# Channel sums of a two-layer banded kernel: four classes of 32 channels on the array's column quarters instead of two halves of 64

## Chip, cores and metric

The kernel runs on one core of a Trainium2 chip. The metric is device time in microseconds (us) of one execution; lower is better. "Before" is the median of three runs.

## What is computed

Input x has 512 x 512 positions with 64 channels, fp32. Two layers of the same kind follow each other, each adding its result to its input. Cut to what matters:

```python
def _gn(v, G=32, eps=1e-5):            # groups of two channels
    g = v.reshape(B_, H_, W_, G, C_ // G)
    m = jnp.mean(g, axis=(1, 2, 4), keepdims=True)
    s = jnp.var(g, axis=(1, 2, 4), keepdims=True)
    return ((g - m) / jnp.sqrt(s + eps)).reshape(v.shape)

# one layer, on xn = _ln(_gn(x)) with 64 channels, HID = 128
left  = (xn @ Wl + bl) * mask * sigmoid(xn @ Wlg + blg)
right = (xn @ Wr + br) * mask * sigmoid(xn @ Wrg + brg)
out_gate = sigmoid(xn @ Wog + bog)
out = _banded_ingoing(left, right, 4)  # 9 products per output, along one axis
out = _ln(out) * out_gate
x = x + (out @ Wo + bo)
```

`_gn` needs, for each of 32 groups of two channels, the mean and the variance over all 512 x 512 positions. For the second layer these are statistics of the first layer's output, and the second layer can't begin before they are complete.

## The kernel before, in words

The 512 rows are cut into nine overlapping blocks of 64 (`row_blocks`), the other axis into chunks; a **unit** (`Unit`, `Out`) is 64 rows by 8 positions of either half of the axis, so that 128 partitions hold two halves. There are 288 units a layer, 8 to a **period**, 36 periods. Before the first layer `input_stats` reads the whole input once on VectorE for the first `_gn`, while the weights are prepared (`solve_layer`, `save`).

A unit goes through some thirty **steps**: `load`, `scale`, `move` (the affine map of `_gn`), `inner` and the steps to `resc` (the layer norm), `ztr`, `keep` (transposes on TensorE, copies on ScalarE), `proj`, `sig`, `right` (projections and their gate), `band` (the banded products, `mix`), `copy`, `ost`, `norm`, `turn`, `gate`, `gated`, `tg` and `last` (`end`, the product with Wo), then `end` (the addition to x in tile XR), `stp` (store) and, in the first layer alone, `sums`. The order in which the engines get the steps of a period is written out by hand in the tables `FIRST` (line 39, first layer) and `SECOND` (line 69); every engine works in the order of its program. In `FIRST` stand eight `sums` steps, one per unit of the period.

`sums` (line 902) adds each finished unit to the statistics of the first layer's output, without leaving TensorE: the tile XR (line 1231) holds, for each of up to 128 partitions (one row of one half), four pairs of neighbouring positions, 2 x 64 channels each, with a column of ones on either side (`clear_xr`, line 1234; `fetch`, line 865, places the data between them). The matrix product of the 64 channels of one position with themselves and the ones has the sums of squares on its diagonal and the channel sums in the column of ones. It accumulates over all units in one PSUM tile, `acc` (line 1242): positions of even place in its lower 64 partitions, of odd place in the upper 64. A unit is 4 x 2 fp32 matmuls with contraction over the rows, 64 stationary columns and 65 moving columns:

```python
acc[t * D : (t + 1) * D], lhsT=o.xr[:n, k, 1 + t * D : 1 + (t + 1) * D],
rhs=o.xr[:n, k, t * (D + 1) : (t + 1) * (D + 1)],
```

The profile's rows count each fp32 matmul as two records of a matmul, with a weight load (LDWEIGHTS) to each; a transpose is one record.

After the first layer `mid_stats` (line 1134) takes the diagonal and the sums out of `acc`, adds the part of the bias bo (`bo_col`, loaded in `save`, line 1182), sums the partitions of one group by a matmul with the tile `same` (line 202), and makes the affine map of the second layer's `_gn`.

Of the kernel before, what the change touches and what calls it, by code (L numbers as in the profile page):

```python
# [10 lines left out]
F32 = mybir.dt.float32  # L11
# [3 lines left out]
ALU = mybir.AluOpType  # L15
# [4 lines left out]
P = 128  # L20
# [4 lines left out]
JU = 8  # L25
# [5 lines left out]
NX = 6  # L31
# [2 lines left out]
NB = 32  # L34
GN_EPS = 1e-5
LN_EPS = 1e-6
UP = (1024.0 / 27.0) ** 2

FIRST = """
# [77 lines left out]
def col(v: bass.AP) -> bass.AP:  # L117

    return v.rearrange("(p o) -> p o", o=1)
# [38 lines left out]
def tile_two_banded_layers(  # L158
# [6 lines left out]
    nc = tc.nc  # L165
    _, L, _, D = x.shape
# [7 lines left out]
    sm = ctx.enter_context(tc.tile_pool(name="sm", bufs=2))  # L174
# [19 lines left out]
    ident = const.tile([P, P], F32, name="ident")  # L194
# [3 lines left out]
    ln_eps = const.tile([P, 1], F32, name="ln_eps")  # L198
    nc.vector.memset(ln_eps, LN_EPS * UP)
    ones_row = all_ones[:1]  # L200

    same = const.tile([P, D], F32, name="same")
    nc.vector.tensor_tensor(same, ident[:, :D], ident[:, D:], ALU.add)
    pair = const.tile([P, G], F32, name="pair")
    nc.vector.tensor_reduce(pair, same.rearrange("p (g t) -> p g t", t=2), AX.X, ALU.add)
    nc.vector.tensor_scalar(
# [8 lines left out]
    def any_bank():  # L215
        return two_banks(next(turns))[:, :512]
# [59 lines left out]
    def strided(v: bass.AP, at: int, *dims) -> bass.AP:  # L276

        return bass.AP(tensor=v.tensor, offset=v.offset + at, ap=[list(d) for d in dims])
# [35 lines left out]
    def solve_layer(i: int, f: dict, r: dict, tmp, half: bass.AP):  # L314
# [67 lines left out]
        en.vector.tensor_tensor(r["m2"], r["m"], r["m"], ALU.mult)  # L382
        en.vector.tensor_scalar(r["m2"], r["m2"], UP / H, None, ALU.mult)

# [13 lines left out]
    bo = [const.tile([P, D], F32, name="bo0"), None]  # L398
    bo_col = const.tile([P, 1], F32, name="bo_col")
# [7 lines left out]
    def group_affine(mean: bass.AP, var: bass.AP, pool):  # L407

        ve = pool.tile([P, D], F32, name="g_ve")
        nc.vector.tensor_scalar(ve, var, GN_EPS, None, ALU.add)  # L410
        rsqrt(ga, ve, pool)
        nc.vector.scalar_tensor_tensor(gb, mean, -1.0, ga, ALU.mult, ALU.mult)
# [328 lines left out]
    def solve(w: dict, ins: list, outs: list, sti, sto) -> tuple:  # L741
# [19 lines left out]
        def prepare():  # L761
            held.extend((work[0], temporary("var")))
            bank, v = held
            if ni:
                en.scalar.activation(
                    pairs(v[:, :ni]), sti[:, : ni // 2, 2::3], AF.Identity, bias=ln_eps,
                    scale=UP / D,
                )
# [7 lines left out]
        def seed():  # L776
            bank, v = held
            y = bank[:, :n]
            if no:
                vo = bank[:, 6 * NB : 6 * NB + no]  # L780
                vec.tensor_tensor(vo, vo, w["m2"][:, js], mult)
                vec.tensor_scalar(v[:, ni:], vo, LN_EPS * UP, None, add)

# [77 lines left out]
    def rows_of(v: bass.AP, o: Out, e: int):  # L861
        b, j = o.blk, e * LH + o.j
        return v[b.s + b.lo : b.s + b.hi, j : j + JU, :].rearrange("p (k t) c -> p k (t c)", t=2)

    def fetch(src: bass.AP, o: Out, n: int, stats: bool):
        o.xr = XR[n % NX]
        if stats:
            o.f = o.xr[:, :, 1 : 1 + 2 * D]
        else:
            o.f = o.xr.rearrange("p k c -> p (k c)")[:, : JU * D].rearrange("p (k c) -> p k c", c=2 * D)  # L870
        for e in range(2):
            en.sync.dma_start(o.f[e * S : e * S + o.blk.m], rows_of(src, o, e))
# [29 lines left out]
    def sums(o: Out, first: bool, final: bool):  # L902


        n = S + o.blk.m
        for k in range(JU // 2):
            for t in range(2):
                en.tensor.matmul(
                    acc[t * D : (t + 1) * D], lhsT=o.xr[:n, k, 1 + t * D : 1 + (t + 1) * D],
                    rhs=o.xr[:n, k, t * (D + 1) : (t + 1) * (D + 1)],  # L910
                    start=first and k == 0, stop=final and k == JU // 2 - 1,
                )

    def layer(src: bass.AP, dst: bass.AP, w: dict, stats: bool, then=None):
# [15 lines left out]
        if stats:  # L930
            for n in range(2):
                posts.setdefault(n - 1, []).append(lambda n=n: clear_zh(ZH[n]))
            for n in range(NX):
                posts.setdefault(n, []).append(lambda n=n: clear_xr(XR[n]))
        posts.setdefault(0, []).append(keep_left)
# [198 lines left out]
    def mid_stats(sm):  # L1134

        sums = sm.tile([P, 2], F32, tag="t_sums", name="t_sums")
        sq = sm.tile([P, D], F32, tag="t_sq", name="t_sq")
        for t, at in enumerate((0, D)):
            part, c = slice(t * D, (t + 1) * D), slice(1 - t, 1 - t + D)
            nc.vector.tensor_copy(sums[part, 0:1], acc[part, at : at + 1])  # L1140
            nc.vector.tensor_tensor(sq[part], acc[part, c], ident[part, part], ALU.mult)
        nc.vector.tensor_reduce(sums[:, 1:2], sq, AX.X, ALU.add)
        n = L * L / 2.0
        own = sm.tile([P, 2], F32, tag="t_own", name="t_own")
        nc.vector.tensor_scalar(own[:, 0:1], bo_col, n, None, ALU.mult)
        nc.vector.tensor_tensor(own[:, 0:1], own[:, 0:1], sums[:, 0:1], ALU.add)
        nc.vector.tensor_tensor(own[:, 1:2], own[:, 0:1], sums[:, 0:1], ALU.add)
        nc.vector.tensor_tensor(own[:, 1:2], own[:, 1:2], bo_col, ALU.mult)
        nc.vector.tensor_tensor(own[:, 1:2], sums[:, 1:2], own[:, 1:2], ALU.add)
        sums = own  # L1150
        rhs = sm.tile([P, 2, D], F32, tag="t_rhs", name="t_rhs")
        for i in range(2):
            nc.vector.tensor_scalar(rhs[:, i, :], same, sums[:, i : i + 1], None, ALU.mult)
        pm = any_bank()[:, : 2 * D]
        nc.tensor.matmul(
            pm, lhsT=all_ones, rhs=rhs.rearrange("p i c -> p (i c)"), start=True, stop=True
        )
        ev = sm.tile([P, 2 * D], F32, tag="t_ev", name="t_ev")
        nc.vector.tensor_copy(ev, pm)
        var = sm.tile([P, D], F32, tag="t_var", name="t_var")  # L1160
        nc.vector.tensor_tensor(var, ev[:, :D], ev[:, :D], ALU.mult)
        nc.vector.tensor_tensor(var, ev[:, D:], var, ALU.subtract)
        nc.vector.tensor_scalar(var, var, 0.0, None, ALU.max)
        nc.vector.tensor_tensor(ev[:, :D], ev[:, :D], bo[0], ALU.subtract)
        group_affine(ev[:, :D], var, sm)
# [4 lines left out]
    with tc.tile_pool(name="setup", bufs=1) as tmp:  # L1170

        half = tmp.tile([P, P], F32, name="half")
        nc.vector.memset(half, 0.0)
        for e in range(2):
            nc.vector.memset(half[e * D : (e + 1) * D, e * D : (e + 1) * D], 1.0 / D)
        got = [fetch_layer(i, v, tmp) for i, v in enumerate(layers)]
        later_pack = tmp.tile([P, n_pack], F32, name="later_pack")
        solved = [w, views(later_pack)]
        for i, r in enumerate(solved):
            r["left"] = tmp.tile([P, 2 * H], F32, name=f"left{i}")  # L1180

        def save():
            rest = tmp.tile([P, D], F32, name="rest")
            en.vector.tensor_tensor(rest, bo[0], bo[1], ALU.add)
            for n in range(3):
                piece = tmp.tile([P, D], BF16, name=f"piece{n}")
                en.vector.tensor_copy(piece, rest)
                nc.gpsimd.dma_start(pieces[n : n + 1], piece[:1])
                en.vector.tensor_tensor(rest, rest, piece, ALU.subtract)
            for i, r in enumerate(solved):  # L1190
                nc.gpsimd.dma_start(left_w[i], r["left"])
            nc.gpsimd.dma_start(spare, later_pack)
            for n in range(2):
                nc.gpsimd.dma_start(bo_col[n * D : (n + 1) * D], col(layers[0]["bo"]))
            yield

        def meanwhile(t: int):

            if t > 1:
                next(solving, None)  # L1200

        def work_of():
            for i in range(2):
                yield from solve_layer(i, got[i], solved[i], tmp, half)
            yield from save()

        solving = work_of()

        def afterwards():
            for _ in solving:  # L1210
                pass
            next(one)
            for z in left_of.rearrange("a (p m w) -> a p m w", p=P, w=WIDE):
                en.sync.dma_start(z, mid(nothing, z.shape[1]))

        input_stats(meanwhile, afterwards)


    keep = ctx.enter_context(tc.tile_pool(name="keep", bufs=1))
# [8 lines left out]
        "p (h n t) -> p h n t", h=H // 2, t=2  # L1228
    )

    XR = [keep.tile([P, JU // 2, 2 * D + 2], F32, name=f"XR{i}") for i in range(NX)]
    ZH = [keep.tile([H, 2, JU, S], F32, name=f"ZH{i}") for i in range(2)]

    def clear_xr(t: bass.AP):
        en.vector.memset(t, 0.0)
        for at in (0, 2 * D + 1):
            en.vector.memset(t[:, :, at : at + 1], 1.0)

    def clear_zh(t: bass.AP):
        en.scalar.copy(t.rearrange("h n x p -> h (n x p)"), mid(nothing, 2 * JU * S // WIDE))  # L1240

    acc_bank = psa.tile([P, 512], F32, name="acc")
    acc, work = acc_bank[:, : D + 1], [acc_bank[:, P:]]


    ztp = ctx.enter_context(tc.tile_pool(name="ztp", bufs=1))
# [41 lines left out]
```

## Time and profile before

| | us |
|---|---|
| median of three runs | 4223.51 |
| lowest and highest run | 4216.28, 4238.14 |
| the profiled execution, its own time | 4215.75 |
| its span in the trace | 4214.0 |
| busy: PE, PEld, DVE, ACT, POOL | 3733.6, 3201.5, 3679.0, 3315.6, 3576.5 |

PE is the matmuls of TensorE, PEld its weight loads (they overlap the matmuls), DVE VectorE, ACT ScalarE, POOL GpSimd, SP the engine that issues most transfers. Nearly all instructions are recorded through one helper, so their line is that of the helper (L491); groups are told apart by their tiles, written out<-in. Tiles: `acc` the statistics, `XR` the unit with x added, `bank<-pack,ZH` the product with Wo in `end`, `banks<-pack,ZT` and `banks<-pack,zT` the projections, `banks<-ZT,pack` the gates, `banks<-ident,z` and `banks<-ident,on` the transposes, `banks<-RO,A` the banded products, `z` the unit being normalised, `RO` right and the banded result, `gn_st` the input statistics. A shape like `64*128 64x448` on TensorE is contraction rows by stationary columns, then rows by moving columns.

The share of the span that an engine is busy averages over input statistics, first layer (about 380 to 2243 us) and second layer. "issue" is time in which an engine waited for nothing that the profile shows. In the chain (the work that ended last, followed back from the end) a piece is a stretch of one kind of work with the number of instructions in it; it begins when the piece before it ended.

### The profile page before, as it was taken

What the parts mean: (1) busy time and instruction counts of PE and PEld (TensorE: products, weight loads), DVE (VectorE), ACT (ScalarE), POOL (GpSimd) and SP (SyncE); (2) the same over time, 40 slices, a digit from 0 to 9 for tenths busy, and PEclk for the clock granted to TensorE, in tenths of its full rate; (3) what the DMA queues carried; (4) which work ended last, traced back from release to release, by engine and by line L of the source; (5) the groups of instructions that cost most, each with busy time, mean ns of one, the idle gap of its engine ahead of it and who ended that gap; (6) DMA issues with size and microseconds to landing.
All of it is one profiled execution on the core that took longest, in us unless ns stands there. A gap on an engine that the chain in (4) does not pass through costs nothing.

```text
span 4214.0 us, 222743 instructions
## 1 busy us (share of the span) xinstructions
PE 3733.6 (89%) x94986; PEld 3201.5 (76%) x94986; DVE 3679.0 (87%) x9911; ACT 3315.6 (79%) x6372; POOL 3576.5 (85%) x4566
## 2 busy tenths in 40 slices
PE   0159999999999999999995899999999999999998
PEld 0047888888888888887874788888878888888886
DVE  8968888888888888888877899998989899999997
ACT  0037888888888888888873788888889888988897
POOL 2368998999998999998945799999989999999983
PEclk9979999999999999999997999999999999999999
DMA  9843646464646464645434454646364646464633
GB/s 398 330 104 93 154 115 147 118 152 115 154 116 152 117 149 113 151 121 136 125 103 113 104 148 123 156 122 155 119 152 120 155 118 158 117 154 119 159 109 95
DMA packets 691107, 596.21 MB, mean 141 GB/s; under 512 B 133702, under 2 KB 545382, under 8 KB 687812
## 3 DMA queue, kind: packets, MB, share of 16 engines
q1 hardware_dynamic: 687604, 580.41, 50.7%
q8 instruction: 748, 12.26, 1.2%
q14 instruction: 243, 1.99, 0.2%
q0 software_dynamic: 2512, 1.56, 0.1%
HBM read 436.71 MB, written 149.74 MB: 139 GB/s over the span
## 4 chain that ended last, share of the span: by engine, by line
PE 80%; DVE 6%; issue 5%; DMA 4%; POOL 4%; ACT 2%; SPq 0%; POOLq 0%; DVEq 0%; ACTq 0%
PE banks L491 61%; PE bank L491 15%; PE acc L491 4%; POOL z L491 3%; DVE gn_st L491 2%; DMA z<-mid_x 1%; DVE z L491 1%; DVE RO L491 1%; DVE ZH L491 1%; DVE sto L491 1%; POOL on L491 1%; DMA nb<-in_L_conv_norm_bias_dram 0%; DMA raw<-in_L_conv_Wrg_dram 0%; DMA brow<-in_L_conv_bl_dram 0%; DMA brow<-in_L_conv_br_dram 0%
## 5 line engine op out<-in xcount | busy, mean ns | idle before, releaser
L491 ACT ACTIVATE on<-RO,nm,rs 128x128 f32<-128x128 f32 x2484 | 1144.4, 499 | 134.3 <-PE banks L491 119.8
L491 POOL TENSOR_SCALAR on<-RO,rs,nm 128x128 f32<-128x128 f32 x2124 | 949.9, 458 | 347.9 <-PE banks L491 302.3
L491 PE MATMUL banks<-pack,ZT 64*128 64x128 f32 x9216 | 995.6, 286 | 26.9 <-DVE RO L491 11.1
L491 PE MATMUL banks<-pack,zT 64*128 64x128 f32 x9216 | 944.3, 276 | 9.9 <-issue 8.8
L491 DVE TENSOR_TENSOR RO<-banks,sg 128x512 f32<-128x512 f32 x1152 | 777.0, 684 | 165.8 <-ACT sg L491 142.9
L491 PEld LDWEIGHTS banks<-pack,ZT 64*128 64x128 f32 x9216 | 761.4, 190 | 150.0 <-ACT zT L491 36.0
L491 DVE BATCH_NORM_STATS2 sto<-RO 128x6 f32<-128x256 f32 x2304 | 852.2, 412 | 3.4 <-ACT RO L491 3.4
L491 ACT ACTIVATE sg<-banks 128x512 f32<-128x512 f32 x1170 | 691.0, 595 | 173.1 <-PE banks L491 135.7
L491 DVE SCALAR_TENSOR_TENSOR ZH<-banks,pack,ZH 128x896 f32<-128x896 f32 (+1 forms) x576 | 667.3, 1159 | 152.1 <-PE banks L491 104.0
L491 PE MATMUL banks<-RO,A 64*64 64x64 f32 x36864 | 699.1, 223 | 111.7 <-issue 106.0
L491 PEld LDWEIGHTS banks<-RO,A 64*64 64x64 f32 x36864 | 623.9, 136 | 213.2 <-issue 148.4
L491 POOL TENSOR_TENSOR z<-z,ga 128x512 f32<-128x512 f32 x556 | 718.8, 1293 | 63.6 <-DMA z<-mid_x 26.2
L491 PEld LDWEIGHTS banks<-pack,zT 64*128 64x128 f32 x9216 | 745.9, 191 | 12.8 <-issue 10.4
L491 POOL TENSOR_TENSOR z<-z,gb 128x512 f32<-128x512 f32 x556 | 716.1, 1288 | 3.5
L491 PE MATMUL bank<-pack,ZH 128*64 128x64 f32 x18432 | 663.2, 225 | 20.7 <-DVE ZH L491 11.1
L491 PEld LDWEIGHTS bank<-pack,ZH 128*64 128x64 f32 x18432 | 590.0, 138 | 111.0 <-issue 56.4
L491 ACT COPY RO<-banks 128x1024 f32<-128x1024 f32 x540 | 542.2, 1011 | 149.4 <-PE banks L491 140.1
L491 POOL TENSOR_TENSOR z<-z,rs 128x512 f32<-128x512 f32 x586 | 615.0, 1056 | 47.7 <-DVE rs L491 45.4
L491 POOL TENSOR_TENSOR z<-z,sti 128x512 f32<-128x512 f32 x586 | 620.1, 1068 | 36.0 <-DVE sti L491 32.0
L491 ACT ACTIVATE ZH<-banks 128x896 f32<-128x896 f32 (+1 forms) x576 | 535.1, 929 | 80.5 <-PE bank L491 56.1
L491 PE MATMUL banks<-ZT,pack 64*128 64x448 f32 (+1 forms) x2304 | 574.6, 574 | 3.3 <-DVE ZH L491 1.4
L491 DVE BATCH_NORM_STATS2 sti<-z 128x6 f32<-128x128 f32 x2344 | 509.2, 281 | 61.7 <-POOL z L491 60.8
(202 smaller groups left out, 4051.1 us busy)
## 6 DMA issues: line engine op xcount, KB each, us to landing
z<-in_x_dram SPq DMA_DIRECT2D x576, 128.0 KB
A<-left_of SPq DMA_DIRECT2D x288, 256.0 KB
z<-mid_x SPq DMA_DIRECT2D x576, 128.0 KB
gn_x<-in_x_dram SPq DMA_DIRECT2D x16, 4096.0 KB
XR<-in_x_dram SPq DMA_DIRECT2D x448, 112.0 KB
mid_x<-XR SPq DMA_DIRECT2D x448, 112.0 KB
XR<-mid_x SPq DMA_DIRECT2D x448, 112.0 KB
out_dram<-XR SPq DMA_DIRECT2D x448, 112.0 KB
```

What stands on the lines that cost most here:

```text
L491: return lambda *a, **k: tc.keep_in_program_order(f(*a, **k))
```

## The change

The 128 columns of a pair of positions are dealt to four classes: class r takes every fourth column from r on, 32 columns, 16 of either position. Each class is multiplied with itself and one column of ones, 32 stationary by 33 moving columns, into its own 32 partitions of `acc`. XR's row becomes 128 data columns followed by four columns of ones, so that one stride of four reaches the class and its ones; data now begin at column 0. `mid_stats`, `same` and `bo_col` follow the new placing of channels on partitions: `bo_col` is loaded by eight small transfers instead of two.

```diff
--- before.py
+++ after.py
@@ -34,6 +34,8 @@
 NB = 32
 GN_EPS = 1e-5
 LN_EPS = 1e-6
+SC = 4
+CG = P // SC
 UP = (1024.0 / 27.0) ** 2
 
 FIRST = """
@@ -200,7 +202,10 @@
     ones_row = all_ones[:1]
 
     same = const.tile([P, D], F32, name="same")
-    nc.vector.tensor_tensor(same, ident[:, :D], ident[:, D:], ALU.add)
+    halves = ident.rearrange("p (r h i) -> p h i r", r=SC, h=2)
+    nc.vector.tensor_tensor(
+        same.rearrange("p (i r) -> p i r", r=SC), halves[:, 0], halves[:, 1], ALU.add
+    )
     pair = const.tile([P, G], F32, name="pair")
     nc.vector.tensor_reduce(pair, same.rearrange("p (g t) -> p g t", t=2), AX.X, ALU.add)
     nc.vector.tensor_scalar(
@@ -865,7 +870,7 @@
     def fetch(src: bass.AP, o: Out, n: int, stats: bool):
         o.xr = XR[n % NX]
         if stats:
-            o.f = o.xr[:, :, 1 : 1 + 2 * D]
+            o.f = o.xr[:, :, : 2 * D]
         else:
             o.f = o.xr.rearrange("p k c -> p (k c)")[:, : JU * D].rearrange("p (k c) -> p k c", c=2 * D)
         for e in range(2):
@@ -904,10 +909,10 @@
 
         n = S + o.blk.m
         for k in range(JU // 2):
-            for t in range(2):
+            for r in range(SC):
                 en.tensor.matmul(
-                    acc[t * D : (t + 1) * D], lhsT=o.xr[:n, k, 1 + t * D : 1 + (t + 1) * D],
-                    rhs=o.xr[:n, k, t * (D + 1) : (t + 1) * (D + 1)],
+                    acc[r * CG : (r + 1) * CG], lhsT=o.xr[:n, k, r : 2 * D : SC],
+                    rhs=o.xr[:n, k, r::SC],
                     start=first and k == 0, stop=final and k == JU // 2 - 1,
                 )
 
@@ -1134,11 +1139,11 @@
     def mid_stats(sm):
 
         sums = sm.tile([P, 2], F32, tag="t_sums", name="t_sums")
-        sq = sm.tile([P, D], F32, tag="t_sq", name="t_sq")
-        for t, at in enumerate((0, D)):
-            part, c = slice(t * D, (t + 1) * D), slice(1 - t, 1 - t + D)
-            nc.vector.tensor_copy(sums[part, 0:1], acc[part, at : at + 1])
-            nc.vector.tensor_tensor(sq[part], acc[part, c], ident[part, part], ALU.mult)
+        sq = sm.tile([P, CG], F32, tag="t_sq", name="t_sq")
+        nc.vector.tensor_copy(sums[:, 0:1], acc[:, CG:])
+        for r in range(SC):
+            part = slice(r * CG, (r + 1) * CG)
+            nc.vector.tensor_tensor(sq[part], acc[part, :CG], ident[part, part], ALU.mult)
         nc.vector.tensor_reduce(sums[:, 1:2], sq, AX.X, ALU.add)
         n = L * L / 2.0
         own = sm.tile([P, 2], F32, tag="t_own", name="t_own")
@@ -1191,7 +1196,12 @@
                 nc.gpsimd.dma_start(left_w[i], r["left"])
             nc.gpsimd.dma_start(spare, later_pack)
             for n in range(2):
-                nc.gpsimd.dma_start(bo_col[n * D : (n + 1) * D], col(layers[0]["bo"]))
+                for r in range(SC):
+                    at = r * CG + n * CG // 2
+                    nc.gpsimd.dma_start(
+                        bo_col[at : at + CG // 2],
+                        strided(layers[0]["bo"], r, (SC, CG // 2), (1, 1)),
+                    )
             yield
 
         def meanwhile(t: int):
@@ -1228,19 +1238,18 @@
         "p (h n t) -> p h n t", h=H // 2, t=2
     )
 
-    XR = [keep.tile([P, JU // 2, 2 * D + 2], F32, name=f"XR{i}") for i in range(NX)]
+    XR = [keep.tile([P, JU // 2, 2 * D + SC], F32, name=f"XR{i}") for i in range(NX)]
     ZH = [keep.tile([H, 2, JU, S], F32, name=f"ZH{i}") for i in range(2)]
 
     def clear_xr(t: bass.AP):
         en.vector.memset(t, 0.0)
-        for at in (0, 2 * D + 1):
-            en.vector.memset(t[:, :, at : at + 1], 1.0)
+        en.vector.memset(t[:, :, 2 * D :], 1.0)
 
     def clear_zh(t: bass.AP):
         en.scalar.copy(t.rearrange("h n x p -> h (n x p)"), mid(nothing, 2 * JU * S // WIDE))
 
     acc_bank = psa.tile([P, 512], F32, name="acc")
-    acc, work = acc_bank[:, : D + 1], [acc_bank[:, P:]]
+    acc, work = acc_bank[:, : CG + 1], [acc_bank[:, P:]]
 
 
     ztp = ctx.enter_context(tc.tile_pool(name="ztp", bufs=1))
```

The tables `FIRST` and `SECOND` are the same, and no step moves. One place of TensorE's program, around two units of sums in the middle of the first layer, before:

```order
L491 MATMUL banks<-ident,z 128x64 x8
L491 MATMUL acc<-XR_1085 64x65 x8
L491 MATMUL bank<-pack,ZH_1090 64x64 x16
L491 MATMUL acc<-XR_1086 64x65 x8
L491 MATMUL banks<-ident,on 128x64 x16
```

and the same place after the change:

```order
L496 MATMUL banks<-ident,z 128x64 x8
L496 MATMUL acc<-XR_1091 32x33 x16
L496 MATMUL bank<-pack,ZH_1096 64x64 x16
L496 MATMUL acc<-XR_1092 32x33 x16
L496 MATMUL banks<-ident,on 128x64 x16
```

(Shapes here are stationary by moving columns, one row a matmul of the program and not yet two records; the numbers behind XR and ZH are buffers.) Nothing stands elsewhere; each unit of sums is 16 matmuls where it was 8. Counted over the layer, `bank<-pack,ZH` follows directly behind 144 of the 288 units of sums and stands directly ahead of 72, in both programs.

## Rows read from the trace of the kernel before

**Rows 1.** The page, parts 1 and 4: busy times, chain by engine.
```profile
PE 3733.6 (89%) x94986; PEld 3201.5 (76%) x94986; DVE 3679.0 (87%) x9911; ACT 3315.6 (79%) x6372; POOL 3576.5 (85%) x4566
...
PE 80%; DVE 6%; issue 5%; DMA 4%; POOL 4%; ACT 2%; SPq 0%; POOLq 0%; DVEq 0%; ACTq 0%
```
**Rows 2.** Windows: stretch, length, busy (xinstructions) of PE PEld DVE ACT POOL, clock, DMA.
```profile
1000.00:1400.00 400.00, 386.61 (x10294) 336.93 (x10287) 346.58 (x926) 341.27 (x651) 369.13 (x474) 1.00 0.54 133
```
**Rows 3.** Waits of TensorE and of GpSimd, 600 to 2100 us: total, times, longest.
```profile
PE banks L491 <- issue: 46.9, 62, 2.5
PE banks L491 <- POOL z L491: 4.0, 4, 1.6
...
POOL on L491 <- PE banks L491: 114.5, 43, 8.3
```
**Rows 4.** Tile acc: duration ns minimum/median/maximum, first and last start, shapes.
```profile
L491 PE MATMUL acc<-XR x4608: 217/222/372, 375.9 to 2242.7; 120*64 120x65 f32 x150, 124*64 124x65 f32 x42
```
**Rows 5.** Chain, from 1012 us: start, length in us, what.
```profile
1012.45 1.08 PE bank L491 x32
1013.53 0.47 PE acc L491 x16
...
1017.48 0.62 PE acc L491 x16
1018.10 0.93 PE bank L491 x32
```
**Rows 6.** Timeline of TensorE's matmuls: start, length in us, what, records.
```profile
1015.29 0.39 PE L491 MATMUL banks<-pack,ZT 64*128 64x128 f32 x4
...
1017.07 0.41 PE L491 MATMUL banks<-ident,z 64*128 64x64 f32 x8
...
1040.72 2.15 PE L491 MATMUL banks<-RO,A 64*64 64x64 f32 x128
1042.80 1.02 PE L491 MATMUL banks<-ZT,pack 64*128 64x448 f32 x4
```
**Rows 7.** The page, part 3: a queue of instruction packets: packets, MB, share.
```profile
q8 instruction: 748, 12.26, 1.2%
```
**Rows 8.** Chain, 1312 to 1330 us: the pauses called issue.
```profile
1312.48 0.74 issue
...
1316.79 0.41 issue
...
1320.45 1.04 issue
1321.49 3.14 PE banks L491 x127
1324.63 2.37 issue
```
**Rows 9.** Chain, two pauses that follow each other after 1104 us.
```profile
1104.89 1.61 issue
...
1109.79 0.18 issue
```
**Rows 10.** Windows: one period, from a unit of sums to its successor.
```profile
1013.37:1064.89 51.52, 51.20 (x1384) 44.90 (x1381) 46.20 (x125) 45.45 (x88) 49.54 (x63) 1.00 0.45 119
```
**Rows 11.** Tile bo_col: the two transfers that GpSimd issues, ns.
```profile
L1194 POOL DMA_DIRECT2D bo_col<-in_L_conv_bo_dram x2: 545/564/584, 112.3 to 124.8; - x2
```
**Rows 12.** Timeline of GpSimd: a gather of the input statistics, its wait in brackets.
```profile
154.91 0.40 POOL L491 TENSOR_TENSOR gn_off<-gn_st 128x64 f32<-128x64 f32 x1 [9.55 <-DVE gn_st L491]
```
**Rows 13.** Tile acc: the products that take the diagonal, between the layers.
```profile
L1141 DVE TENSOR_TENSOR on<-acc,ident x2: 207/218/229, 2243.1 to 2243.5; 64x64 f32<-64x64 f32 x2
```
**Rows 14.** The page, part 5: busy, mean ns of one, idle before.
```profile
L491 DVE BATCH_NORM_STATS2 sto<-RO 128x6 f32<-128x256 f32 x2304 | 852.2, 412 | 3.4 <-ACT RO L491 3.4
...
L491 DVE BATCH_NORM_STATS2 sti<-z 128x6 f32<-128x128 f32 x2344 | 509.2, 281 | 61.7 <-POOL z L491 60.8
```


## Prediction

> **What bounds the kernel now.** I read the page first, then the windows, the waits, the chain and at last single steps in the timeline. The page [rows 1] shows TensorE busy for 89% of the span and on 80% of the chain that ended last. The sums are issued in the first layer alone, so I looked at that layer by itself. In the 400 us from 1000 us TensorE is busy for 386.6 us at a granted clock of 1.00; GpSimd follows with 369.1, VectorE has 346.6, ScalarE 341.3 [rows 2]. The waits say who holds whom: in 1500 us of that layer TensorE's longest waits for another engine come to 4.0 us, and 46.9 us go to "issue", that is, for nothing the profile shows; GpSimd in turn waits 114.5 us for TensorE [rows 3]. So the first layer takes as long as TensorE takes, pauses included, and a gain or a loss there of one or two per cent passes through whole: GpSimd has over 7% of room before it would bind. The second layer issues no sums, and nothing in it changes.
>
> **What the sums cost now.** There are 4608 records of matmuls [rows 4], each with its weight load (the page counts as many loads as matmuls [rows 1]). With 288 units of 8 matmuls that is two pairs of load and matmul for each fp32 matmul: 16 pairs a unit. The chain shows a unit of sums as 0.47 us where it follows the matmuls of `end` and as 0.62 us where it follows another shape; the matmuls of `end` take 1.08 us after another shape and 0.93 us behind sums [rows 5]. Both have 64 output columns, so they share a layout of the array. From this I read two prices. A **change of layout** costs 0.15 us. And the **streaming**: 0.47 us for 8 groups of two neighbouring pairs is 58 ns a group, as is 0.93 us for 16 groups in `end`: the two column halves run side by side.
>
> **The price of a quarter group.** The projections stream 128 columns in groups of two: 8 runs of 4 records take 1017.07 - 1015.29 = 1.78 us, 111 ns a group of two [rows 6]. Between 64 and 128 columns lie 53 ns, 0.83 ns a column with some 5 ns on top; 33 columns would then take 32.5 ns. Four tiles side by side exist in this trace: the band products (64 by 64) do 128 records, 32 groups of four, in 1042.80 - 1040.72 = 2.08 us [rows 6]; without the layout change that is 60 ns a group, as fast as a group of two. So I take 32.5 ns for a group of four quarters. The upper end is four passes one after another, 4 x 32.5 = 130 ns; the lower end is the same 32.5, since no row shows a column below 0.83 ns.
>
> **The sum, over the layer.**
> - Streaming: 288 units x 8 groups, before and after (16 matmuls are 32 pairs in groups of four). 2304 x (58 - 32.5 ns) = **-59 us**; at 130 ns +166 us.
> - Layout: in the order of TensorE's program `end` follows directly behind 144 of the 288 units of sums and stands directly ahead of 72. These 216 places have no change of layout now. With 32 columns beside 64 they get one: 216 x 0.15 = **+32 us**. No row shows 32 columns, so the lower end is 0; but the nearest rows pay it [rows 5], so I take it whole.
> - Instructions: 16 more pairs a unit, 288 x 32 = 9216 more instructions. Instructions come in packets: 748 packets with 12.26 MB [rows 7] are 16.4 KB each; 748 x 256 instructions would be 191 thousand, and TensorE's loads and matmuls are 190 thousand [rows 1], so this queue is TensorE's. In the chain the "issue" pauses stand 127 to 128 matmuls apart, with their weight loads 256 instructions [rows 8]: a pause is the wait for the next packet. Between the ends of neighbouring pauses lie 3.98, 4.29 and 5.51 us, elsewhere 3.47 us [rows 8, 9]: a mean of 4.3 us that a packet needs where TensorE takes instructions as fast as they come. One period of eight units holds 1384 matmul records in 51.52 us, 10.8 packets or 4.8 us each [rows 10]; after the change it is 1512, 11.8 packets or 4.4 us each. The supply, invisible on most of the period now, has nearly no room left. The pauses are 46.9 us in 1500 [rows 3], 1.6 us a period. If they only grow with the number of packets they gain 9%, 0.15 us a period or +5 us in 36 periods. If they grow as the room shrinks, from about 0.5 to 0.1 us, they more than double: over +1.6 us a period, +58 us or more. Seven of the eight units stand outside the band products, where the pauses gather; I take growth by half, 0.8 us a period, **+29 us**.
> - Setup: six more small DMAs from GpSimd at 0.56 us each, 3.4 us [rows 11]. They stand amid the gathers of the input statistics, and GpSimd later waits 9.55 us for VectorE there [rows 12], so they are covered; uncovered they would cost 3.4 us.
> - Between the layers: two copies and two products of 64 x 64 become one copy and four products of 32 x 32; a product takes 0.22 us [rows 13], so at most 0.4 us more. The last units of sums before it are shorter by about as much. XR's clearing loses one small memset per buffer. The new offset of XR touches transfers that nobody on the chain waits for. All of it: 0.
> The sum is -59 + 32 + 29 = **+2 us** on the profiled execution's 4215.75 us. That one lies 7.8 us under the median of the three runs, 4223.51; against the median I forecast **4226 us**. The three runs spread over 0.5%, and about 0.5%, 21 us, is what a measurement of this kernel can tell from no change.
>
> **Rivals.**
> 1. *The strided operand streams at half the rate* (slower). Both operands now take every fourth fp32, 16 bytes apart. The band products step by 8 bytes and lose nothing (60 against 58 ns), so the trace is silent at 16. If a column takes twice as long, a group takes 5 + 2 x 27.5 = 60 ns: streaming costs +5 us in place of -59, the layout change stays at +32, and pauses grow less, say +10, since the steps are not denser: +47 us, 4270 us. It decides from a group of 41 ns on: 2304 x 8.5 ns are the 19 us up to the forecast's upper edge. The same time comes if dispatch binds: the fastest row is 60 ns for four pairs, and nothing shows four pairs sustained in 32.5. For the rival: no row with that step on TensorE. Against it: VectorE reads z with neighbouring elements in different tokens, 256 bytes apart, in 281 ns for 128 elements, and RO in 412 ns for 256 [rows 14]; with the same fixed part that is 1.02 ns an element for both, not double.
> [...]
> [...]
> 2. *The quarters do not run side by side* (slower). If the four passes share one stream, or contend for one partition's reads, a group takes up to 130 ns: +166 + 32 = +198 us, 4420 us; two at a time, 65 ns, is rival 1. Then the change does not do what its words say. Against it: halves do run side by side, and so do the four tiles of the band products; but there only two tiles read the same partitions.
> 3. *The supply keeps up, or quarters and halves are one layout* (faster). With pauses at +5 us: -59 + 32 + 5 = -22 us, 4202 us. With no layout change either: -54 us, 4170 us. For it: over a period the packets still fit, 4.4 against 4.3 us. Against it: the mean leaves no room for the long ones (5.51 us), and a stretch with two units and `end` between them takes 96 pairs nearly at once.
>
> **How the numbers follow.** The forecast, within 21 us of no change, gets 0.46: the unit does get shorter, and the layout changes and the supply take it back. Rival 1 gets 0.26, rival 2 0.10, rival 3 0.18. Faster by over 0.5% is most of rival 3 (its -22 us stands on the edge) and a little of the forecast: 0.16. Slower is rivals 1 and 2 and the forecast's upper edge, where the pauses double: 0.39. Same is 0.45. The range of 8 in 10 leaves out rival 2 and the far half of rival 3 and keeps rival 1 with its spread: 4188 to 4290 us; the forecast's own is 4205 to 4250.
>
> **What would show it.** The sums' row has 9216 records of 33 columns. Right would be: a unit alone in the chain at about 0.26 us behind its first group instead of 0.47; `end` behind sums at 1.08 us and no longer 0.93; "issue" waits in 600 to 2100 us near 70 instead of 46.9 us; a period still near 51.5 us; other engines' busy time unchanged. A unit of 0.5 us or more is rival 1, of 1 us rival 2; `end` still at 0.93 us behind sums or issue waits still below 52 us is rival 3. I am wrong at the root if TensorE begins to wait for another engine in the first layer, or if the second layer's time moves.

## The result: slower by 1.4%, and the profile after

| | before | after |
|---|---|---|
| median, us | 4225.27 | 4283.66 |
| lowest and highest of four runs | 4216.28, 4238.14 | 4273.61, 4294.79 |
| the profiled execution | 4215.75 | 4273.61 |
| last start of a sum, us | 2242.7 [rows 4] | 2296.8 |

The ratio is 1.0136, 95% interval 1.0098 to 1.0175: the changed kernel is slower, by 58 us. Of the 57.9 us between the two profiled executions 53 lie in the first layer (first to last sum, 375.9 to 2242.7 before, 376.7 to 2296.8 after). The number lies in the range that was given; the forecast, no difference that can be measured, did not come true. That the range holds it is owed to rival 1, which the range was drawn to keep; the forecast's own range ended at 4250.

The page of the changed kernel, parts 1, 3 and 4, to be read beside [rows 1, 7]:
```profile
PE 3767.2 (88%) x99594; PEld 3223.0 (75%) x99594; DVE 3684.2 (86%) x9906; ACT 3323.3 (78%) x6372; POOL 3590.9 (84%) x4572
...
q8 instruction: 784, 12.85, 1.3%
...
PE 80%; DVE 7%; issue 5%; DMA 4%; POOL 2%; ACT 2%; SPq 0%; DVEq 0%; POOLq 0%; ACTq 0%
```
TensorE has 4608 more matmul records and as many more weight loads, 9216 instructions, and its queue 36 more packets, 256 instructions each, as worked out. TensorE still carries the chain, and its busy time has grown by 34 us where it should have fallen.

Tile acc of the changed kernel, matmuls and weight loads (columns as in [rows 4]):
```profile
L496 PE MATMUL acc<-XR x9216: 222/247/265, 376.7 to 2296.8; 120*32 120x33 f32 x153, 124*32 124x33 f32 x44
...
L496 PEld LDWEIGHTS acc<-XR x9216: 134/159/181, 376.7 to 2296.7; 120*32 120x32 f32 x153, 124*32 124x32 f32 x44
```
This row points to it first: a matmul of 33 columns has a median of 247 ns, one of 65 columns had 222 [rows 4]. Half the columns take longer, be it for the step or for the four tiles; e1 tells which.

Its chain from 1037 us:
```profile
1037.75 0.67 PE acc L496 x27
1038.42 1.08 PE bank L496 x32
1039.50 0.67 PE acc L496 x28
```
A unit of sums takes 0.67 us, behind `end` as elsewhere, where it took 0.47 or 0.62 [rows 5]; `end` behind sums takes 1.08, where it took 0.93. (A piece counts the records that lie on the chain; tile acc above has all 9216.) With 0.15 us of the 0.67 for the layout, eight groups take 0.52 us: **65 ns a group of four quarters**, not 32.5. In the single records of the unit at 1033.5 us the four matmuls of a group start within some 20 ns, and then the next group waits until 65 ns are over: it is not the issuing of four pairs that takes the time.

Waits of TensorE, 600 to 2100 us, after:
```profile
PE banks L496 <- issue: 54.0, 70, 2.4
PE bank L496 <- issue: 1.5, 1, 1.5
PE acc L496 <- issue: 0.8, 3, 0.3
PE banks L496 <- DVE RO L496: 0.5, 2, 0.4
```
and two rows of the same view before, which with [rows 3] make 48.3 us:
```profile
PE acc L491 <- issue: 0.7, 1, 0.7
PE bank L491 <- issue: 0.7, 1, 0.7
```
Windows of that stretch (columns as in [rows 2]), before:
```profile
600.00:2100.00 1500.00, 1446.20 (x38452) 1262.64 (x38450) 1297.11 (x3463) 1278.00 (x2429) 1384.20 (x1761) 1.00 0.53 133
```
and after:
```profile
600.00:2100.00 1500.00, 1441.84 (x40860) 1252.21 (x40863) 1266.14 (x3370) 1249.87 (x2372) 1355.33 (x1718) 1.00 0.52 130
```
The matmul records count the periods in it: 38452 / 1384 = 27.78 before, 40860 / 1512 = 27.02 after. A period went from 54.0 to 55.5 us. (The 51.52 us of [rows 10] were a short one.) The other engines lose busy time in proportion; they are simply slowed down. The granted clock is the same, 1.00.

These rows make an account, per period of eight units:
- sums: before 2 units of 0.47 and 6 of 0.62, 4.66 us; after 8 x 0.67 = 5.36. **+0.70**, of it 2 x 0.15 for the layout;
- `end`: 144 / 36 = 4 times 0.15. **+0.60**;
- issue: 48.3 / 27.78 = 1.74 before, 56.3 / 27.02 = 2.08 after. **+0.34**.

Together 1.64 us, in 36 periods 59 us, against 57.9 measured between the two executions. By cause: layout 0.90 x 36 = +32, streaming 0.40 x 36 = +14, supply +12.

### The profile page after: what moved, and what is told of

It is laid out like the page before. It is cut to its first block, busy times and chain, and to the rows that moved or that the text cites. A ratio compares the mean times of both kernels' runs of the same rounds, so it can differ in the third digit from the quotient of the medians.

```text
span 4271.8 us, 231960 instructions
## 1 busy us (share of the span) xinstructions
PE 3767.2 (88%) x99594; PEld 3223.0 (75%) x99594; DVE 3684.2 (86%) x9906; ACT 3323.3 (78%) x6372; POOL 3590.9 (84%) x4572
## 3 DMA queue, kind: packets, MB, share of 16 engines
q8 instruction: 784, 12.85, 1.3%
## 4 chain that ended last, share of the span: by engine, by line
PE 80%; DVE 7%; issue 5%; DMA 4%; POOL 2%; ACT 2%; SPq 0%; DVEq 0%; POOLq 0%; ACTq 0%
PE banks L496 60%; PE bank L496 15%; PE acc L496 4%; POOL z L496 2%; DVE gn_st L496 2%; DMA z<-mid_x 1%; DVE RO L496 1%; DMA raw<-in_L_conv_Wr_dram 1%; DVE sto L496 1%; DVE ZH L496 1%; DVE z L496 1%; DMA A<-left_of 1%; ACT sg L496 1%; DMA raw<-in_L_conv_Wl_dram 0%; DMA brow<-in_L_conv_brg_dram 0%
## 5 line engine op out<-in xcount | busy, mean ns | idle before, releaser
L496 PE MATMUL banks<-pack,ZT 64*128 64x128 f32 x9216 | 989.9, 285 | 31.3 <-DVE RO L496 16.4
```

The source lines that it names most:

```text
L496: return lambda *a, **k: tc.keep_in_program_order(f(*a, **k))
```

## The experiments

Theory "step": the group takes 65 ns because neighbouring columns of an operand lie 16 bytes apart. Rivals: four pairs cannot be dispatched faster, four quarters contend, or the supply sets the pace. Times are medians of interleaved runs, ratios are to the kernel before in the same runs; "per period" is worked out as above.

**e1: neighbouring columns.** The changed kernel with the quarters cut as stretches:
```diff
-                    acc[r * CG : (r + 1) * CG], lhsT=o.xr[:n, k, r : 2 * D : SC],
-                    rhs=o.xr[:n, k, r::SC],
+                    acc[r * CG : (r + 1) * CG], lhsT=o.xr[:n, k, r * CG : (r + 1) * CG],
+                    rhs=o.xr[:n, k, r * CG : (r + 1) * CG + 1],
```


> The changed kernel with both operands of a quarter taken as neighbouring columns (32 and 33) instead of every fourth. It leaves the statistics wrong: the 33rd column is ones only in the last class, and the placing of channels is not followed. Same number of matmuls, same shapes, same quarters. Theory 'step' (16 bytes between elements slows the streaming): a unit in the chain falls from 0.67 to about 0.42 us (8 groups of 33 ns and a layout change), the matmul's row from 247 to about 200 ns; with layout changes and supply as in the changed kernel 4200 to 4225 us. Theory 'four' (four tiles reading the same partitions, or dispatch, set 65 ns a group): unit 0.67 us and about 4283 us as in the changed kernel.

Measured: 4263.18 against 4232.32, ratio 1.0073 [1.0052, 1.0095], +31 us. Tile acc:
```profile
L496 PE MATMUL acc<-XR x9216: 190/196/247, 375.5 to 2276.1; 120*32 120x33 f32 x153, 124*32 124x33 f32 x44
...
L496 PEld LDWEIGHTS acc<-XR x9216: 105/110/162, 375.5 to 2276.1; 120*32 120x32 f32 x153, 124*32 124x32 f32 x44
```
Its chain:
```profile
1029.14 0.39 PE acc L496 x32
1029.54 1.08 PE bank L496 x32
```
Its waits and its window:
```profile
PE banks L496 <- issue: 74.1, 82, 2.4
PE acc L496 <- issue: 3.6, 4, 1.5
PE bank L496 <- issue: 3.6, 4, 1.8
```
```profile
600.00:2100.00 1500.00, 1412.63 (x41273) 1212.61 (x41272) 1275.21 (x3404) 1253.49 (x2391) 1360.86 (x1730) 0.99 0.53 132
```
The unit is 0.39 us, 0.24 without the layout: about 31 ns a group, the price forecast. So four quarters do run side by side and four pairs can be dispatched in 31 ns; only the step stood in the way of the streaming, 65 ns with it. And yet the kernel is still slower than before, and 38 us above the upper end that was expected. The pauses in the row "issue" went from 48.3 to 81.3 us: over 41273 / 1512 = 27.30 periods that is 2.98 us each, +1.24 a period, **+45 us**, where the units give back (8 x 0.39 - 4.66) x 36 = -55 and `end` takes 22. These rows leave +12 of the +34 us by which the first layer grew between the profiles (375.5 to 2276.1 us here); some 20 us stand in none of these rows.

Counted record by record over the whole layer of both traces (the time from the end of one matmul to the end of the next, put down to the later one), the sums go from 168.1 to 113.6 us, `end` from 290.3 to 313.0, the pauses from 56.0 to 96.3, and all other matmuls of TensorE from 1333.0 to 1355.2: there the missing time lies, 7.9 us of it in the band products and 5.9 in the transposes of z. Why those take longer is open. The clock is not enough: the clock records of the traces have two levels, full and half, and TensorE is at half for 34 us of e1's layer and for 17 us of that before (mean granted clock 0.991 and 0.995), which is 8.5 us at most, and e2 below has a layer 32 us longer than before at a mean of 0.996.

**e2: a step of 8 bytes.** Classes of every second channel of one position, ones at either end:
```diff
+                at = r // 2 * D + r % 2
...
+                    acc[r * CG : (r + 1) * CG], lhsT=o.xr[:n, k, 2 + at : 2 + at + 2 * CG - 1 : 2],
```


> Quarters with a step of two elements, 8 bytes: class is (position, even or odd channel), two columns of ones ahead of the 128 and two behind. Computes the reference. [...] Theory 'step', any step costs in proportion: between, unit near 0.53 us, 4245 us. Theory 'four': unit 0.67 us, 4283 us.

Measured: 4261.18, ratio 1.0072 [1.0052, 1.0091]. Chain:
```profile
1026.32 0.42 PE acc L496 x29
```
0.42 against 0.39 us: a step of 8 bytes costs about 4 ns a group, one of 16 bytes some 34 (65 against 31). A cost in proportion, between the 0.39 us of e1 and the 0.67 of the changed kernel, would have been 0.53. The total is 36 us above the 4225 that was the upper end for e1, much as in e1 and in the same terms (over the whole layer the pauses take 98.5 us, the other matmuls 1348.0).

**e3: the halves of before with a step of 16 bytes.** No quarters, no layout change, no more instructions:
```diff
+                at = k // 2 * 4 * (D + 2) + k % 2 * 2 + t
...
+                    acc[t * D : (t + 1) * D], lhsT=flat[:n, at : at + 4 * D - 3 : 4],
+                    rhs=flat[:n, at : at + 4 * D + 1 : 4],
```


> The kernel before, two halves of 64 stationary and 65 moving columns, but both operands step by four elements (16 bytes) over two pairs of positions; it leaves the statistics wrong. [...] Theory 'four': a step alone costs nothing with two tiles: unit 0.47 us, 4225 us.

Measured: 4349.2, ratio 1.0278 [1.0259, 1.0298], +117 us. Tile acc and two pieces of the chain:
```profile
L491 PE MATMUL acc<-XR x4608: 290/302/377, 377.6 to 2373.7; 120*64 120x65 f32 x150, 124*64 124x65 f32 x42
```
```profile
1010.15 1.16 PE acc L491 x14
1011.31 0.93 PE bank L491 x32
1012.25 1.01 PE acc L491 x16
```
A unit behind `end` takes 1.01 us where it took 0.47: 126 ns a group of two halves against 58. Twice the time with two tiles, so the step and not the number of tiles; and `end` behind sums stays at 0.93, so the layout is not touched by the step. The units add 0.54 x 288 = 156 us, and 117 of them arrive. Waits of TensorE:
```profile
PE banks L491 <- issue: 35.8, 43, 2.2
```
The pauses fall from 48.3 to 36.0 us in the 1500 (another 0.2 us stand in `bank`), in the whole layer by 13 us; that the slower steps leave the packets more time is an inference from it. The band products take 9 us less as well.

**e5 and e6: the step on one operand alone**, stationary in e5 (first edit of the changed kernel), moving in e6 (second):
```diff
-                    rhs=o.xr[:n, k, r::SC],
+                    rhs=o.xr[:n, k, r * CG : (r + 1) * CG + 1],
```
```diff
-                    acc[r * CG : (r + 1) * CG], lhsT=o.xr[:n, k, r : 2 * D : SC],
+                    acc[r * CG : (r + 1) * CG], lhsT=o.xr[:n, k, r * CG : (r + 1) * CG],
```


> The changed kernel with the step of 16 bytes on the stationary operand alone; the 33 moving columns are neighbours. It leaves the statistics wrong. If loads and matmuls stream side by side and each is slowed by its own step, the slower of the two sets the group: still 65 ns, unit 0.67 us, with the matmul's row near 196 ns and the load's row long. If only the moving operand's step costs: unit 0.39 us as with neighbouring columns on both sides.

> The changed kernel with the step of 16 bytes on the moving operand alone. It leaves the statistics wrong. If each operand is slowed by its own step: unit 0.67 us, the matmul's row near 247 ns, the load's row near 112 ns. If only the stationary operand's step costs: unit 0.39 us.

Measured, one run each: 4278.73 and 4278.87 us, against 4230.75. Tile acc and a piece of the chain of e5:
```profile
L496 PE MATMUL acc<-XR x9216: 190/226/250, 374.6 to 2299.1; 120*32 120x33 f32 x153, 124*32 124x33 f32 x44
...
L496 PEld LDWEIGHTS acc<-XR x9216: 134/157/168, 374.6 to 2299.0; 120*32 120x32 f32 x153, 124*32 124x32 f32 x44
```
```profile
1030.46 0.62 PE acc L496 x32
```
and of e6:
```profile
L496 PE MATMUL acc<-XR x9216: 222/241/256, 376.2 to 2295.7; 120*32 120x33 f32 x153, 124*32 124x33 f32 x44
...
L496 PEld LDWEIGHTS acc<-XR x9216: 105/128/137, 376.2 to 2295.6; 120*32 120x32 f32 x153, 124*32 124x32 f32 x44
```
```profile
1032.08 0.61 PE acc L496 x32
```
The shortest weight load rises from 105 to 134 ns (e1, e5) when the stationary operand is stepped, the shortest matmul from 190 to 222 (e1, e6) when the moving one is: each operand pays by itself some 30 ns (29 and 32), about once more the time of its 32 columns (27 ns by the forecast's 0.83 ns a column). But loads and matmuls overlap, so either one alone already sets the pace (0.62 and 0.61 us a unit), and both together add only 0.05. So the 0.67 us that was expected for each is missed by 0.05, and the medians of the operand without a step rise too (226 against 196, 128 against 110). Taking the step from one operand would have given back 0.05 x 288 = 14 us of the units and left the kernel slower than before.

**e4: no sums but the first and last unit**, in the kernel before, to see what time on TensorE is worth:
```diff
-                sums(outs[t], len(summed) == 1, len(summed) == len(outs))
+                if len(summed) in (1, len(outs)):
+                    sums(outs[t], len(summed) == 1, len(summed) == len(outs))
```


> The kernel before without the sums of all units but the first and the last; it leaves the statistics wrong. What the sums cost in all, and whether a shorter TensorE passes through. If TensorE alone binds: per period 4.66 us of sums go and four changes of layout (0.60) come back to the product with Wo: -4.1 us, 36 periods -146 us, about 4078 us. If GpSimd (49.5 us busy of 51.5 us) binds next: at most 2 us a period, 4150 us or more.

Measured: 4181.39, ratio 0.988 [0.9864, 0.9896], -51 us. Waits of TensorE:
```profile
PE banks L491 <- issue: 41.2, 58, 2.6
PE banks L491 <- ACT zT L491: 33.0, 56, 0.7
PE banks L491 <- POOL on L491: 8.7, 24, 0.4
PE banks L491 <- POOL z L491: 8.2, 25, 0.7
```
TensorE issues 4.66 - 4 x 0.15 = 4.06 us less a period, 146 us in all, and a third of that arrives, as the second of the two expectations has it (4150 us or more). It now waits for ScalarE's copies (`zT`) and for GpSimd, 50 us in 1500 where there were some 4 [rows 3]. Here a gain does not pass through whole, whatever room the busy times show.

**e8: quarters of neighbouring columns over half the positions**, so that the number of instructions is that of before:
```diff
-        for k in range(JU // 2):
+        for k in range(0, JU // 2, 2):
```


> Quarters with neighbouring columns, but of the four pairs of positions only two: 16 pairs of load and matmul a unit, as many instructions as before the change, with the layout changes of the quarters. It leaves out half of the statistics. Theory 'supply' (the extra packets of instructions take back what the quarters save): pauses at packet ends fall from 3.9 to at most 2.5 us a period, the unit from 0.39 to 0.27 us, and the time falls by far more than the 35 us of the shorter unit, from 4263 to 4205 us or less. Theory 'no supply' (what the quarters save is lost elsewhere): the shorter unit alone, about 4228 us, pauses as with 32 pairs.

Measured: 4212.93 against 4230.75, ratio 0.9947 [0.9929, 0.9965], -18 to -22 us by medians and ratio. Chain and waits:
```profile
1011.37 0.26 PE acc L496 x16
```
```profile
PE banks L496 <- issue: 57.3, 74, 2.4
PE banks L496 <- ACT zT L496: 10.4, 47, 1.4
...
PE acc L496 <- issue: 0.5, 2, 0.3
...
PE bank L496 <- issue: 0.4, 2, 0.2
```
Without the additional instructions the same shapes are 50 us faster than e1, of which the shorter units are (0.39 - 0.26) x 288 = 37. (Four groups fewer take 0.13 us less, 32 ns a group, which leaves 0.13 us of a unit to the layout: the price of 0.15 found in another way.) The pauses fall from 81.3 to 58.2 us in 1500, from 2.98 to 2.09 us a period (the 3.9 and 2.5 of the expectation were counted in another way): 32 us in 36 periods, of which a new wait for ScalarE takes back some 13. That speaks for the supply, but what arrives of it is small; the run lies between the theories.

**e9: twice the instructions without step, quarters or layout change.** The halves of before, each cut into two matmuls of 33 by 33 columns (first and last unit as before):
```diff
+            for h in range(1 if first or final else 2):
...
+                        acc[t * D : t * D + c, : c + (c == D)],
+                        lhsT=o.xr[:n, k, 1 + t * D + h * 31 : 1 + t * D + h * 31 + c],
```


> The kernel before, halves in their layout and neighbouring columns, but each matmul of the sums replaced by two with 33 stationary and 33 moving columns: 32 pairs a unit, as many instructions as with quarters, no change of layout and no step; the first and the last unit stay as they were. It leaves out part of the statistics. 16 groups of two at 33 ns are 0.52 us a unit in place of 0.46: +17 us. Theory 'supply': pauses at packet ends grow from 2.5 to about 3.8 us a period as with neighbouring columns in quarters, another +45 us: about 4290 us, ratio 1.014. Theory 'no supply': the streaming alone, about 4248 us, ratio 1.004, pauses as before.

Measured: 4270.5 against 4229.1, ratio 1.0094 [1.0074, 1.0114], +41 us. Three pieces of the chain, the waits and the window:
```profile
1039.12 0.52 PE acc L491 x32
...
1043.12 0.64 PE acc L491 x32
1043.76 0.96 PE bank L491 x32
```
```profile
PE banks L491 <- issue: 67.5, 83, 2.2
PE acc L491 <- issue: 4.1, 4, 2.2
PE bank L491 <- issue: 1.4, 2, 1.0
```
```profile
600.00:2100.00 1500.00, 1423.20 (x40838) 1244.87 (x40836) 1265.51 (x3369) 1245.71 (x2370) 1348.20 (x1716) 0.99 0.53 130
```
The unit is 0.64 us behind another shape and 0.52 behind `end`, and `end` behind sums 0.96: behind 33 columns `end` pays 0.03 us more than its 0.93 where a change of layout costs 0.15, and the work itself has grown by 6 x 0.02 + 2 x 0.05 + 4 x 0.03 = 0.34 us a period, +12 us. The pauses are 73.0 us over 40838 / 1512 = 27.01 periods, 2.70 each: +0.96 a period, +35 us. Together +47, within the interval of the ratio (+31 to +48). Here little but the number of instructions has changed, and it costs 35 us in the pauses, 29 by the medians (41 less 12, with some 9 either way): the cost of the supply is shown by itself. Where the pauses stand says the same: from one pause of over 0.2 us to the next, e9 has 58 distances below 1100 instructions of TensorE (loads and matmuls) in the 1500 us, and every one is one to four times 252 to 256; so are all 62 in e1 and all 34 before.

**e10: the layout change alone.** The halves of before with the contraction cut to 64 rows, as many instructions as before, no step:
```diff
-        n = S + o.blk.m
+        n = S
```


> The kernel before with the sums' contraction cut to the 64 rows of one half: same number of matmuls, same 64 and 65 columns, same step, but half the rows, so that sums and the product with Wo no longer share a layout. It leaves out half of the statistics. If a change of layout costs 0.15 us and passes through: sums always 0.62 us, the product with Wo always 1.08 us, 216 x 0.15 = +32 us, ratio 1.0077. If other engines' room hides it: ratio below 1.004. If only the columns of a tile make a layout and not its rows: nothing changes, ratio 1.000.

Measured: 4255.74 against 4229.1, ratio 1.0066 [1.005, 1.0083], +27 us. Chain, and the longest wait:
```profile
1025.99 0.61 PE acc L491 x16
1026.61 1.08 PE bank L491 x32
1027.69 0.61 PE acc L491 x16
```
```profile
PE banks L491 <- issue: 49.5, 65, 2.3
```
`end` takes 1.08 us behind sums and the unit 0.61 behind `end`, with pauses nearly as before. 8 x 0.61 - 4.66 + 0.60 = 0.82 us a period are 30 us: the price of 0.15 us a change holds, and it arrives in the total.

**e7: fewer layout changes.** In `FIRST`, the two units of sums that stood alone are moved, one beside another unit, one ahead of `last`:
```diff
-sums:-1 tg:1 ost3:5 move:7 ost0:5 keep0:1 keep1:1 norm6:2 scale:11 band:1@2 ost1:7 proj0:1@0
+tg:1 ost3:5 move:7 ost0:5 keep0:1 keep1:1 norm6:2 scale:11 band:1@2 ost1:7 proj0:1@0
...
-resc:8 resc:10 sums:4 norm3:8 proj1:7@1 ztr:8@0 norm5:8! sums:5 norm6:8 sig1:7 end:6 keep0:8
+resc:8 resc:10 norm3:8 proj1:7@1 ztr:8@0 norm5:8! sums:4 sums:5 norm6:8 sig1:7 end:6 keep0:8
```


> The kernel before with two of the eight sums of a period moved so that every sums stands beside the product with Wo or beside another sums; computes the reference. Three changes of layout a period fewer, 0.45 us, 36 periods -16 us if TensorE's time passes through: ratio 0.996. If other engines or the supply of instructions take it: ratio 1.000.

Measured: 4241.73 against 4230.75, ratio 1.0022 [1.0006, 1.0038], +9 us: nothing gained, a little lost. Waits of TensorE:
```profile
PE banks L491 <- issue: 40.5, 58, 1.8
PE banks L491 <- ACT zT L491: 10.9, 24, 1.0
PE banks L491 <- POOL on L491: 6.8, 21, 0.4
```
What the layout gave, some 16 us by its price, went into waits for ScalarE and GpSimd, as in e4. Whether they come of the earlier matmuls or of the new order itself this run does not tell. None of the versions that keep the statistics whole beats the kernel before, and no run pointed to one that would.

## Why the prediction was right or wrong, step by step

- **What bounds the kernel: right.** In the stretch of the first layer that was looked at, TensorE still waits for no other engine but for half a microsecond at a time, and 53 of the 58 us arose in that layer. The sentence that a gain **or a loss** passes through whole did not hold for gains, and for losses only in part: e10 lost 27 us of the 30 of its account, e3 117 of 156, e4 gained a third of its 146, e7 nothing of its 16. Room in busy time was read as slack; it is not, since ScalarE's `zT` and GpSimd are late at single places where TensorE is earlier (33.0 and 16.9 us in 1500 in e4; with the new order of e7 10.9 and 6.8).
- **The price of a quarter group: the step that failed.** "So I take 32.5 ns for a group of four quarters": it was 65, and with it the streaming term became +14 us instead of -59. The 32.5 itself was read well: with neighbouring columns the chip gave 31 (e1). What was wrong was to let it stand for operands with a step of 16 bytes. Rival 1 named this mechanism and gave 60 ns and 4270 us; e1, e2, e3, e5 and e6 show it, from both sides. The evidence against it was VectorE's reads at a wide step; it did not carry over to TensorE. The price by 60 ns was 4270; 65 ns add 2304 x 5 ns = 12 us, nearly the distance to 4283.66. The runs have two steps alone: 8 bytes cost 4 ns a group (e2 against e1), 16 bytes 34 (the changed kernel against e1). What makes the difference between the two no run shows.
- **The layout: right**, +32 us forecast, +32 in the account, and e10 alone gave +27 against the 30 of its own account.
- **The supply: right in kind, too large for this kernel.** +29 was forecast, +12 came, because the growth was worked out for dense steps and the steps were not dense; rival 1 had +10 for that case. The room was also read from the one short period of 51.52 us: with the mean of 54.0 a packet had 5.0 us before and would have had 4.6, not 4.8 and 4.4. Where the steps are dense the forecast was too small: +45 in e1, +35 in e9. Rival 3 is out on both its grounds: the pauses grew, and the layout changes were paid. That a packet of this queue holds 256 of TensorE's instructions came out as worked out: 9216 more of them took 36 more packets, and 12.85 MB in 784 packets are again 16.4 KB each.
- **Rival 2 (four passes one after another): out**, by e1's 31 ns a group of four: its unit starts 32 pairs in about 0.24 us, 8 ns apart.
- **Setup, statistics between the layers, the second layer: right**, all within the 4 to 5 us that the rest of the span grew by.

Taken together, the forecast was a balance of a gain against two losses, of which the layout was sized well, the supply too high for this kernel, and the gain was not there. Even with the gain the balance would not have been even: e1, which is the change as it was priced, is 31 us slower than before. Why the other matmuls take some 22 us longer in e1 stays open, as does why a stepped group takes 65 ns and not the 60 of doubled columns.

## What to carry to other kernels

Before a matmul's operand is given a step, measure that step on TensorE itself: here fp32 operands at a step of 8 bytes kept nearly full pace (about 4 ns more on a group of 31, e2 and e1) and at 16 bytes halved it (65; with one operand alone stepped the unit took 0.62 and 0.61 us against 0.39, e5 and e6), and VectorE's rows did not tell it. Smaller matmuls also cost here what their columns do not show: a packet for every 256 instructions (36 for 9216), and a change of layout of 0.15 us where shapes of another kind stood next to them; count both before the columns. And of time freed on the busiest engine a part arrived here, of time added most: 51 of 146 us against 27 of 30 and 117 of 156.

## What the hardware showed that was not expected

- On average four tiles' pairs start 8 ns apart (e1: 32 in 0.24 us), half of the 16 ns of the band products, the closest that the kernel before showed (128 records in 2.08 us [rows 6]); with 33 columns in place of 64 the spacing halved, so dispatch did not set those 16 ns.
- A contraction cut to 64 rows costs what 32 columns cost (`end` behind sums 1.08 us in e10 as in e1, 0.93 before), while 33 columns beside 64 cost little of it (0.96 in e9).
- A stepped stationary operand slows the weight load by as much as a stepped moving one slows the matmul: the shortest by 29 ns (105 to 134, e5) and by 32 (190 to 222, e6).
